# A list scheduler without same-engine waits, with another port rule and a margin on its costs, for a one-core RWKV and local-attention kernel

## The chip, the cores and the metric

The kernel runs on one core of one Trainium2 chip, in float32. The metric is the device time in microseconds (us) of one execution of the whole program. Each version is run several times and the median counts.

The core has five engines that matter here: TensorE (PE, matrix products and transposes), VectorE (DVE), ScalarE (ACT), GpSimd (POOL) and SyncE (SP, which issues all DMA transfers of this kernel). Each engine takes its instructions strictly in the order in which the program lists them, and waits on semaphores for the results of the others.

## The reference, cut to what matters

The input x is 2 x 4096 x 256. Two residual blocks follow each other. The first is an RWKV mixer: layer norm, three projections of a token-shifted input, a recurrence over the 4096 positions, a group norm, and an output projection.

```python
x = x + rwkv(layernorm(x))        # r, k, v projections, scan over time, group norm, W_o
x = x + ffn(layernorm(x))         # two layers of the following
```

Each of the two layers of the second block has local attention in windows of 128 positions, where a query sees its own and the previous window, and a gated feed-forward:

```python
h = shift_token(x)                          # second half of the channels one position later
q, k, v = split(h @ wqkv, 3)                # 8 heads of 64
q, k = rotary_xpos(l2norm(q) * qs, l2norm(k) * ksc)
o = softmax(mask(8 * q @ k_around.T)) @ v_around
x = x + o @ wo
h = layernorm(shift_token(x)) * lg + lb
a, g = split(h @ w1 + b1, 2)                # 682 hidden channels
x = x + (a * gelu(g)) @ w2 + b2
```

## The kernel before

The kernel is written as a recording. Every call such as `nc.vector.tensor_tensor(...)` does not emit an instruction; `note` (L230) stores it as an operation with its engine, its place in the recording and the earlier operations it depends on. `cost` (L294) gives each operation two figures: `step`, for how long it occupies its engine, and `time`, after which its result is there. It also sets `lock`, which says whether the operation takes the port that VectorE and GpSimd share. When all is recorded, `order` (L364) runs a list schedule over five engines and `give` (L490) emits the operations in the order of their planned starts. All real instructions therefore carry the line of that emission, L506, but for two forms of one operation: L500 (VectorE) and L502 (ScalarE).

`order` keeps for each engine a list of operations whose predecessors are planned. `ready` (L383) says when such an operation could start: after the planned end of each predecessor plus `SEM` = 60 ns. `earliest` (L393) raises this if the shared port is taken or if no PSUM bank is free. Of the operations that could start first on an engine (within 1 ns, L427), the one with the lowest priority key goes, and the key is the row at which the code placed it. The engine whose next start is earliest moves on. Operations recorded on the engine `either` (copies out of PSUM, and `scaled`, a multiplication by a number per partition) have no engine yet; they stand in the lists of both ScalarE and VectorE and go to whichever comes first. In the schedule before, two operations of one engine that depend on each other are also kept apart by the full `time` of the first plus 60 ns; other operations may be planned in between.

The work itself runs in three stages. First the recurrence of batch row 0 runs by itself, in chunks of 512 positions (`Recurrence`, L573: `ahead` loads, normalizes and projects a chunk; `scans`, L726, runs it over time). Then a loop (L1389) goes over 128 windows of 128 positions: 2 batch rows x 2 layers x 32 windows. Each turn n finishes window n and prepares window n+1. Four windows make a block of 512 positions, for which the feed-forward runs in large products. In the first 50 or so of the 128 turns the recurrence of batch row 1 is laid in between as 16 chunks of 256 positions, with its own row n + 0.5. So the first half of the loop carries more work of VectorE than the second.

The operations that the text refers to, by the names in the profile:

- `project` (L941) makes q, k and v of window n+1 (`bank<-wqkv,xT`). `norms` (L989) sums the squares (`rn<-sq`) and takes the inverse root on GpSimd (`rn<-rn,mhalf`); `cosines` (L997) and `rotated` (L1003) finish the rotation on VectorE (`sq<-qk,tab`, `sq<-sq,t`, `qk<-sq,rn`), and GpSimd makes the other part (`t<-qk,tab`).
- `transpose_qk` (L1014) transposes q and k on TensorE (`bank<-mats,qk`) in the next turn, before the scores (`bank<-kT,qT`).
- `softmax` (L1062) runs in four groups of two heads. It writes the scores of the own window over the masked ones of the previous window (`COPY_PREDICATED`) and takes the row extreme (`nmx<-bank`) on VectorE, the exponential with its sum on ScalarE (`pr<-bank,nmx`), then on VectorE the reciprocal of the sums (128x2), a 128x2 addition into the first columns (`pr<-pr`), and two `scaled` on `either` (`pr<-pr,sums`, 128x129).
- `transpose_p` (L1109) transposes the probabilities on TensorE (`bank<-mats,pr`), and `pT`, `pB` leave PSUM for the products with v.
- `output` (L1159) adds the result to x; `shift` (L1171) moves it by one position with DMAs on SP (`h<-x`); then the layer norm (`st`, `mv`, `rs`, `h<-h,mv,rs`), and `transpose_h` (L1196) once a block.

Of the kernel before, what the change touches and what calls it, by code (L numbers as in the profile page):

```python
# [54 lines left out]


SEM = 60
LOAD = 1283
TURN = {"row": 195, "col": 95, "full": 199}
SETS = {AF.Exp: 1, AF.Tanh: 1, AF.Gelu: 2, AF.Ln: 3}  # L60
# [98 lines left out]
class Op:  # L159
    __slots__ = (  # L160
        "eng", "name", "args", "kw", "step", "time", "deps", "after", "left", "at", "ready",
        "set", "lock", "ops", "banks", "uses", "passes", "half", "start", "end", "n", "ins", "outs",
    )


# [8 lines left out]
class Plan:  # L174
# [119 lines left out]
    def cost(self, o):  # L294

        views = [*o.outs, *o.ins]
        n = max([v.idx.size for v in views] or [1])
        psum = any(v.place.psum for v in views)
        wide = sum(v.idx.size > 16 and not v.place.psum for v in o.ins)
        o.set, o.lock, o.half, o.passes, name = None, False, "full", 0, o.name  # L300
        if o.eng == "tensor":
            trans = name == "transpose"
            left = o.args[1]
            move = o.args[2] if len(o.args) > 2 else o.args[1]
            cols = max(move.idx.size, left.idx.size) if not trans else P
            o.step = (1 if trans else 2) * (cols / 1.2 + (2 if cols >= 256 else 3))
            if not trans and left.shape[0] <= 64:
                o.half = "row"
            elif not trans and left.idx.size <= 64:
                o.half = "col"  # L310
            if o.half != "full":
                o.step /= 2
            o.time = o.step + 150
        elif o.eng == "vector":
            d = 150 + 1.04 * n
            if name == "tensor_tensor_reduce":
                d = 240 + 1.04 * n
            elif name == "tensor_tensor_scan":
                d, o.lock = 203 + 2.1 * n, True
            elif name == "scalar_tensor_tensor":  # L320
                d, o.lock = 200 + 1.05 * n, wide > 1
            elif name == "tensor_tensor":
                o.lock = wide > 1
            elif name == "tensor_scalar":
                d, o.lock = 155 + (1.27 if psum else 0.98) * n, not psum and n > 64
            elif name == "tensor_copy" and not psum:
                d, o.lock = 230 + 0.45 * n, n > 64
            elif name == "bn_aggr":
                d = 172
            elif name == "reciprocal":  # L330
                d = 147 + 4 * n
            o.step, o.time = max(d - 85, 60), d
        elif o.eng in ("scalar", "either"):
            d = (160 if psum else 195) + 0.83 * n
            if name == "scaled":
                d = 305 + 0.76 * n
            elif name == "activation":
                o.set = SETS.get(o.args[2])
                if o.args[2] == AF.Identity:
                    d = 365 + 0.87 * n  # L340
                elif isinstance(o.kw.get("bias"), View):
                    d += 85
            o.step, o.time = d - 100, d
            if "accum_out" in o.kw:
                o.time = d + 200
        elif o.eng == "gpsimd":
            o.lock = n > 64
            if name == "tensor_tensor":
                d = 430 + 156 * n if ALU.pow in o.args else 140 + 2.22 * n
            elif name == "tensor_scalar":  # L350
                d = 230 + 1.12 * n
            else:
                d = (100 if name == "memset" else 187) + 0.98 * n
            o.step, o.time = d, d
        else:
            v = min(views, key=lambda v: v.shape[0] * v.idx.size)
            size = 4 * v.shape[0] * v.idx.size
            rows = max(v.shape[0] if v.shape[0] > 1 else v.shape[1] for v in views)
            ways = max(k for k in range(1, 17) if rows % k == 0)
            o.passes = size / 170 if ways == 16 else size / (25 * ways)  # L360
            o.step, o.time = 60, 2000 + o.passes


    def order(self):  # L364
        owner = {}
# [11 lines left out]
        lock = dict.fromkeys(("vector", "gpsimd"), 0.0)  # L377
        waiting = {e: [] for e in engines}
        banks = [0.0] * 8
        counts = {}  # L380
        table, half, dma = 1, "full", 0.0

        def ready(g):  # L383
            t, off = 0.0, 0.0
            for o in g:
                for d in o.deps:
                    if owner[d] is not g:
                        t = max(t, d.end + SEM - off)
                off += o.step
            for e in ("scalar", "vector") if g[0].eng == "either" else (g[0].eng,):  # L390
                waiting[e].append((t, g))

        def earliest(e, t, g):  # L393
# [4 lines left out]
            if need:  # L398
                have = sorted(b for b in banks if b is not None)
                if len(have) < need:  # L400
                    return None
                t = max(t, have[need - 1] + SEM)
            return t
# [8 lines left out]
        while todo:  # L412
            for e in engines:
                if e not in stale:
                    continue
                best = None
                cands = []
                for t, g in waiting[e]:
                    s = earliest(e, t, g)
                    if s is not None:  # L420
                        cands.append((max(s, free[e]), g))
                if not cands:
                    pick[e] = None
                    continue
                t0 = min(s for s, _ in cands)
                for s, g in cands:
                    if s <= t0 + 1:  # L427
                        key = g[0].at
                        if best is None or key < best[0]:
                            best = (key, s, g)  # L430
                pick[e] = (best[1], best[2])
            stale = set()
            e = min((e for e in engines if pick[e]), key=lambda e: pick[e][0], default=None)
            assert e is not None, "no operation can start"
            t, g = pick[e]
            for o in g:
                if e == "tensor" and o.half != half:
                    t += TURN[o.half]
                    half = o.half
                if e == "scalar" and o.set not in (None, table):  # L440
                    t += LOAD
                    table = o.set
                for p in o.banks:
                    b = min((i for i in range(8) if banks[i] is not None), key=lambda i: banks[i])
                    p.bank, banks[b] = b, None
                    p.real = self.bank_tiles[b]
                    counts[p] = (len(p.users), 0.0)
                step, time = o.step, o.time
                if o.eng == "either" and e == "vector":
                    n = o.outs[0].idx.size  # L450
                    time = 150 + 1.04 * n if o.name == "copy" else 155 + 0.98 * n
                    step = time - 85
                    o.lock = o.name == "scaled"
                if o.eng == "either":
                    o.eng = e
                o.start = t
                if e == "sync":
                    dma = max(dma, t) + o.passes
                    o.end = max(t + time, dma + 2000)
                else:  # L460
                    o.end = t + time
                if o.lock and e in lock:
                    lock[e] = o.end
                t += step
                done.append(o)
                for p in o.uses:
                    c, last = counts[p]
                    counts[p] = (c - 1, max(last, o.end))
                    if c == 1:
                        banks[p.bank] = counts[p][1]  # L470
                        stale.add("tensor")
            free[e] = t
            if g[0].lock:
                stale.update(lock)
            stale.add(e)
            for x in engines:
                n = len(waiting[x])
                waiting[x] = [c for c in waiting[x] if c[1] is not g]
                if len(waiting[x]) != n:
                    stale.add(x)  # L480
            for nxt in after.get(id(g), ()):
                left[id(nxt)] -= 1
                if not left[id(nxt)]:
                    ready(nxt)
                    stale.update(("scalar", "vector") if nxt[0].eng == "either" else (nxt[0].eng,))
            todo -= 1
# [1058 lines left out]
```

## Time and profile before

| | |
|---|---|
| median of three runs | 3071.16 us (3068.86 to 3071.94) |
| the profiled execution | 3073.15 us, of which the profile's span is 3071.1 us |
| mean granted TensorE clock in it | 0.991 of full speed |
| TensorE busy, share of the span | 2968.5 us, 97% |
| VectorE | 2609.7 us, 85% |
| ScalarE | 1667.2 us, 54% |
| GpSimd | 1424.4 us, 46% |
| instructions | 48744 |

An engine is busy while an instruction of it runs; waiting on a semaphore does not count. A busy TensorE is not TensorE at its peak, since the ends of its pipelined products are modelled. The page of the profile also follows the chain of work that ended last back from the end, and the queries of the trace give the waits of each engine, the groups of instructions, and the instructions in order of time.

### The profile page before, as it was taken

How to read it: one execution, taken by the hardware profiler on the slowest of the kernel's cores; microseconds unless marked ns; L12 is line 12 of the kernel's file. 1: busy time of each engine (PE TensorE's matmuls, PEld its weight loads, DVE VectorE, ACT ScalarE, POOL GpSimd, SP SyncE). 2: the span in 40 equal slices, each digit the busy share in tenths (PEclk: the TensorE clock that was granted, in tenths of full speed). 3: DMA queues.
4: the chain of work that ended last, by engine and by line, in shares of the span. 5: the costliest groups of instructions: out<-in, count | busy, mean ns of one | idle time of the engine just before them, and what ended most of it. 6: DMA issues, size and time to landing. Idle time of an engine off the chain costs nothing.

```text
span 3071.1 us, 48744 instructions
## 1 busy us (share of the span) xinstructions
PE 2968.5 (97%) x15500; PEld 1914.7 (62%) x15500; DVE 2609.7 (85%) x5969; ACT 1667.2 (54%) x4485; POOL 1424.4 (46%) x1705
## 2 busy tenths in 40 slices
PE   9979999999999999999999999999999999999998
PEld 4456666666666666666666566666666666666665
DVE  7989988989889989898888888888888888888884
ACT  6866755556556566555445454445445445445443
POOL 3227544444445445545544444445444454454440
PEclk9989999999999999999999999999999999999999
DMA  2322112111112111111122221111112121111110
GB/s 82 111 89 68 55 48 64 58 52 49 59 59 66 64 56 59 51 55 50 51 66 78 70 71 58 58 58 56 49 46 69 60 63 56 53 52 55 47 42 24
DMA packets 178313, 182.49 MB, mean 59 GB/s; under 512 B 27044, under 2 KB 147716, under 8 KB 177544
## 3 DMA queue, kind: packets, MB, share of 16 engines
q1 hardware_dynamic: 178056, 179.38, 19.1%
q8 instruction: 123, 2.02, 0.3%
q14 instruction: 134, 1.10, 0.1%
HBM read 79.17 MB, written 33.55 MB: 37 GB/s over the span
## 4 chain that ended last, share of the span: by engine, by line
PE 64%; DVE 22%; ACT 6%; issue 3%; POOL 3%; DMA 1%; SPq 1%; DVEq 0%; ACTq 0%; POOLq 0%
PE bank L506 64%; DVE arena L506 4%; DVE qk L506 2%; ACT pr L506 2%; DVE sq L506 2%; DVE bank L506 2%; DVE rn L506 2%; DVE x L506 2%; DVE pr L500 1%; DVE nmx L506 1%; DVE pB L506 1%; POOL rn L506 1%; ACT L506 1%; ACT arena L506 1%; POOL rs L506 1%
## 5 line engine op out<-in xcount | busy, mean ns | idle before, releaser
L506 PE MATMUL bank<-wqkv,xT 128*128 128x512 f32 x1536 | 727.4, 599 | 0.0
L506 PE MATMUL bank<-hT,w 128*128 128x512 f32 (+1 forms) x1408 | 647.9, 594 | 1.1 <-ACT hT L506 1.1
L506 POOL TENSOR_TENSOR t<-qk,tab 128x256 f32<-128x256 f32 x512 | 379.2, 761 | 443.6 <-DVE qk L506 295.3
L506 ACT ACTIVATE pr<-bank,nmx 128x129 f32<-128x129 f32 (+1 forms) x1024 | 368.5, 375 | 280.6 <-DVE nmx L506 273.3
L506 PEld LDWEIGHTS bank<-hT,w 128*128 128x128 f32 (+1 forms) x1408 | 257.2, 190 | 256.6 <-issue 242.1
L506 PEld LDWEIGHTS bank<-wqkv,xT 128*128 128x128 f32 x1536 | 269.4, 192 | 229.9 <-issue 220.6
L506 POOL TENSOR_TENSOR rn<-rn,mhalf 128x16 f32<-128x16 f32 x128 | 398.0, 3110 | 10.2
L506 PE MATMUL bank<-w,hm 128*128 128x256 f32 x1280 | 288.5, 380 | 0.0
L506 PEld LDWEIGHTS bank<-w,hm 128*128 128x128 f32 x1280 | 242.6, 191 | 33.4 <-issue 1.0
L502 ACT ACTIVATE pr<-pr,sums 128x129 f32<-128x129 f32 (+1 forms) x606 | 225.2, 414 | 52.1 <-DVE pr L506 48.3
L506 PE MATMUL bank<-wo,oT 128*128 128x256 f32 x1024 | 250.0, 387 | 0.2
L506 PE MATMUL bank<-kT,qT 64*128 64x256 f32 (+1 forms) x2048 | 246.9, 381 | 0.0
L506 PEld LDWEIGHTS bank<-mats,pr 128*128 128x128 f32 x1148 | 133.6, 135 | 157.8 <-issue 63.3
L506 PEld LDWEIGHTS bank<-wo,oT 128*128 128x128 f32 x1024 | 188.1, 190 | 69.3 <-issue 35.3
L506 ACT ACTIVATION_READ_ACCUMULATOR pr<-bank,nmx 128x1 f32 x1024 | 217.1, 212 | 0.0
L506 DVE COPY_PREDICATED bank<-packs,bank 128x254 f32<-128x254 int32 x496 | 185.6, 419 | 32.5 <-PE bank L506 32.3
L506 PEld LDWEIGHTS bank<-kT,qT 64*128 64x128 f32 x2048 | 191.1, 187 | 31.8 <-issue 8.4
L506 POOL TENSOR_TENSOR tab<-tab,qks 128x256 f32<-128x256 f32 x128 | 105.2, 822 | 214.7 <-DMA tab<-in_c_rot_dram 201.0
L506 PE MATMUL bank<-pT,vt 128*64 128x128 f32 x2048 | 204.7, 280 | 0.0
L506 PE MATMUL bank<-mats,pr 128*128 128x128 f32 x1148 | 178.0, 276 | 22.4 <-ACT pr L502 15.3
L506 ACT ACTIVATE sq<-qk 128x1024 f32<-128x1024 f32 x128 | 136.0, 1063 | 114.2 <-DVE qk L506 113.1
L506 PE MATMUL bank<-pB,dv 128*64 128x128 f32 x1984 | 194.2, 273 | 3.6 <-DMA pB<-last 2.8
(151 smaller groups left out, 5678.2 us busy)
## 6 DMA issues: line engine op xcount, KB each, us to landing
vr<-vt SPq DMA_DIRECT2D x124, 224.0 KB
tab<-in_c_rot_dram SPq DMA_DIRECT2D x128, 128.0 KB
kT<-kT SPq DMA_DIRECT2D x64, 256.0 KB
z<-zd SPq DMA_DIRECT2D x16, 512.0 KB
x<-in_x_dram SPq DMA_DIRECT2D x16, 512.0 KB
x1d<-x SPq DMA_DIRECT2D x16, 512.0 KB
x<-x1d SPq DMA_DIRECT2D x16, 512.0 KB
h<-x SPq DMA_DIRECT2D x128, 64.0 KB
```

The costliest lines, as they stand in the source:

```text
L500: self.nc.vector.tensor_scalar(dst, src, scale, None, ALU.mult)
L502: self.nc.scalar.activation(dst, src, AF.Copy, scale=scale)
L506: getattr(getattr(self.nc, o.eng), name)(*args, **kw)
```

## The change

The change touches only the planner, not what is computed. It does five things:

1. `ready` counts only predecessors on other engines. An operation that depends on one of its own engine is planned directly behind it, without the 60 ns and without the part of `time` that lies beyond `step`. For `either` operations this is judged for each of the two engines separately.
2. The port rule of VectorE: a two-input operation takes the shared port if both inputs have the full size of the operation and lie in SBUF (before: if both have over 16 elements); one-input forms take it from 17 elements on (before: from 65).
3. The port rule of GpSimd: every operation but `memset` takes the port (before: those of over 64 elements), the small ones only for 100 ns (the new `hold`).
4. The port is held for `hold` from the start, which is the cost without the margin.
5. `SLACK` = 1.06: `step` and `time` of VectorE, ScalarE and GpSimd are multiplied by 1.06 in the plan. TensorE and SP keep theirs.

```diff
+SLACK = 1.06
...
-        wide = sum(v.idx.size > 16 and not v.place.psum for v in o.ins)
-        o.set, o.lock, o.half, o.passes, name = None, False, "full", 0, o.name
+        inside = sum(v.idx.size == n and not v.place.psum for v in o.ins)
+        o.set, o.lock, o.half, o.passes, name, hold = None, False, "full", 0, o.name, None
...
             elif name == "scalar_tensor_tensor":
-                d, o.lock = 200 + 1.05 * n, wide > 1
+                d, o.lock = 200 + 1.05 * n, inside > 1
             elif name == "tensor_tensor":
-                o.lock = wide > 1
+                o.lock = inside > 1
             elif name == "tensor_scalar":
-                d, o.lock = 155 + (1.27 if psum else 0.98) * n, not psum and n > 64
+                d, o.lock = 155 + (1.27 if psum else 0.98) * n, not psum and n > 16
             elif name == "tensor_copy" and not psum:
-                d, o.lock = 230 + 0.45 * n, n > 64
+                d, o.lock = 230 + 0.45 * n, n > 16
...
         elif o.eng == "gpsimd":
-            o.lock = n > 64
+            o.lock = name != "memset"
...
             o.step, o.time = d, d
+            hold = d if n > 64 else 100
...
+        o.hold = hold or o.time
...
         def ready(g):
-            t, off = 0.0, 0.0
-            for o in g:
-                for d in o.deps:
-                    if owner[d] is not g:
-                        t = max(t, d.end + SEM - off)
-                off += o.step
             for e in ("scalar", "vector") if g[0].eng == "either" else (g[0].eng,):
+                t, off = 0.0, 0.0
+                for o in g:
+                    for d in o.deps:
+                        if d.eng != e:
+                            t = max(t, d.end + SEM - off)
+                    off += o.step
                 waiting[e].append((t, g))
...
-                    o.lock = o.name == "scaled"
+                    o.lock, o.hold = o.name == "scaled", time
                 if o.eng == "either":
                     o.eng = e
+                if e not in ("tensor", "sync"):
+                    step, time = step * SLACK, time * SLACK
...
                 if o.lock and e in lock:
-                    lock[e] = o.end
+                    lock[e] = t + o.hold
```

More of the change, by code (lines that the diff above doesn't have):

```diff
@@ L161 @@
         "eng", "name", "args", "kw", "step", "time", "deps", "after", "left", "at", "ready",
-        "set", "lock", "ops", "banks", "uses", "passes", "half", "start", "end", "n", "ins", "outs",
+        "set", "lock", "hold", "ops", "banks", "uses", "passes", "half", "start", "end", "n", "ins", "outs",
     )
```

## The prediction

> **What bounds the kernel now.** I read the page first, for the shares of the engines and of the chain of work that ended last, then the same by stage.
>
> ```profile
> PE 2968.5 (97%) x15500; PEld 1914.7 (62%) x15500; DVE 2609.7 (85%) x5969; ACT 1667.2 (54%) x4485; POOL 1424.4 (46%) x1705
> ...
> PE 64%; DVE 22%; ACT 6%; issue 3%; POOL 3%; DMA 1%; SPq 1%; DVEq 0%; ACTq 0%; POOLq 0%
> ```
>
> TensorE is the bound by busy time, but the chain leaves it for a third of the span, and then it is mostly on VectorE. The windows show where (columns: length, then busy us and instructions by engine):
>
> ```profile
> 0.00:340.00 340.00, 308.28 (x1164) 181.05 (x1165) 297.66 (x625) 241.35 (x473) 143.28 (x213) 0.96 0.26 87
> 340.00:1400.00 1060.00, 1020.66 (x5462) 673.52 (x5461) 957.91 (x2190) 629.22 (x1662) 505.03 (x600) 0.99 0.19 56
> 1400.00:3000.00 1600.00, 1576.54 (x8603) 1021.30 (x8602) 1323.38 (x3089) 778.03 (x2308) 770.30 (x883) 1.00 0.19 58
> ```
>
> While the second recurrence lies between the windows (340 to 1400), VectorE is busy 957.91 of 1060 us, 90%; afterwards 83%. Added up by engine from the chain in order of time, VectorE holds 23% of the chain in the first stage (77 of 340 us), 38% in the second (402 us) and 12% in the third (185 us). An extra microsecond of VectorE is thus worth 0.23, 0.38 and 0.12 us, as long as the chain keeps its course.
>
> What TensorE waits for:
>
> ```profile
> PE bank L506 <- DVE qk L506: 31.1, 31, 2.9
> PE bank L506 <- ACT pr L502: 15.3, 22, 3.4
> ...
> PE bank L506 <- DVE h L506: 9.4, 3, 4.7
> ```
>
> This counts only full idleness. Comparing the starts of successive TensorE instructions with their undisturbed spacing (429 ns at 512 columns, 216 at 256, 109 at 128), I find 158 us lost, by what the late one waited for last: 39 for the q/k transposes (`qk`), 34 for the probabilities (`pr`, `scaled`), 20 for `h`, the rest spread. Of the 39, 18.6 fall on one of the four windows of a block (the second) after turn 56; of the 34, 32.5 on the fourth (21.5 before turn 56, 11.0 after).
>
> **What the Trainium skill says.** "VectorE: DVE Perf Modes", section "The DRAIN you can't avoid", holds that the semaphore between two VectorE operations costs nothing extra. This trace differs:
>
> ```profile
> 1773.49 0.35 DVE L506 TENSOR_TENSOR pr<-pr 128x2 f32<-128x2 f32 x1
> 1773.88 0.91 DVE L500 TENSOR_SCALAR pr<-pr,sums 128x129 f32<-128x129 f32 x2
> 1774.71 0.40 DVE L506 TENSOR_TENSOR x<-x,bank 128x256 f32<-128x256 f32 x1
> ```
>
> The `scaled` needs the addition and starts 0.04 us after its end; the addition to x needs neither and starts 0.08 us before the `scaled` ends. Over the trace the median is +35 ns for 187 adjacent dependent pairs and -83 ns for 4892 independent ones: **a dependent neighbour costs 117 ns of VectorE**. On ScalarE it is +32 against -94, 126 ns; the overlap is the "about 93 ns" of "ScalarE: Activation LUTs", section "What ACT_TABLE_LOAD costs". "SBUF — State Buffer", section "Who interferes with whom", says that a VectorE operation with two SBUF inputs and a GpSimd operation that reads SBUF block each other for the whole instruction. The trace agrees: the 128x2 addition takes 143 ns in the median with GpSimd quiet and up to 1112 ns beside it; such excess sums to 130 us.
>
> **The change part by part.** From the order in which the built programs' instructions stand:
>
> *Dependent neighbours on VectorE.* Adjacent dependent pairs go from 256 to 1529: 495 addition -> `scaled` (81 before), 467 `COPY_PREDICATED` -> reduce (none before), 199 statistics -> aggregate (47), and the steps of the recurrence. The plan used to put another instruction in between. 1273 more x 117 ns = 149 us of VectorE. By stage, cut where the TensorE work before them matches the windows: 174, 486 and 613 pairs, or 20.4, 56.9 and 71.7 us; by the chain shares 4.6 + 21.6 + 8.3 = **+34.5 us**. No trace here shows the pair with `COPY_PREDICATED`. Its bounds are 0 (the skill's page) and 187 ns (the slowest pair shown, addition to addition, +104); 117 is the value of most others. The ends move the total pairs' cost to 94 and 182 us, the sum to +22 and +42.
>
> *Who does the flexible work.* Net 324 `scaled` go from ScalarE to VectorE and 66 copies the other way. A `scaled` on VectorE holds it about 198 ns (281 undisturbed, less 83 of overlap), a copy 597: +64 - 39 = +25 us, nearly all after turn 56, at 0.12: **+3**. ScalarE: -324 x 294 ns + 66 x 490 = -63 us at its chain share of 6%: **-4**. Its 158 more dependent pairs x 126 ns = 20 us: **+1**. Below zero is possible here, as one hop from VectorE to ScalarE goes with each.
>
> *The port.* The 128x2 addition is now kept off GpSimd's time in the plan. It takes 193 ns in the mean against 143, 25 us in all. If half goes, at 22%: **-3**. At worst zero; at best all 130 us of excess at 22%, -29, but most of it is of kinds that both plans keep apart and that overlap all the same.
>
> *Cover.* TensorE's order hardly moves: 96% of adjacent pairs stay, and its turns between half and full array stay 392. But where it moves, it helps. For the second window of a block after turn 56, the TensorE work between `project` and the q/k transposes grows from 10.7 to 13.9 us in the mean, while the VectorE work from `rn` to `qk` grows from 6.8 to 8.9, so 1.1 us is won in 18 blocks; the median cover grows more, from 10.7 to 15.4. I take 13 of the 18.6 us as gone. For the probabilities of the fourth window the cover stays at 7.5 us in the median and VectorE's work before the last `scaled` shrinks from 7.3 to 6.0 us after turn 56 and from 7.2 to 6.8 before: 5 of 32.5. **-18.** The rest stands still or shrinks: in the other windows that VectorE work grows by 1.4 to 2.4 us with the same cover; that is part of the first item. What is late next is again `qk`, in the second stage, where cover grew by 0.6 us and work by 2.0 in the second window.
>
> *Moved at no cost.* The 1496 DMA issues of SP are the same; 64% stand elsewhere, nine in ten by at most three places. The DMAs `h<-x` and what queues behind them on SP hold 2% of the chain in the second stage; other work of TensorE hides them, and if that goes, one late landing costs the 1.95 us that it has in the chain, per block at most: 0 to +30, taken as 0. GpSimd does the same 1701 operations at 46%; it has 71 more dependent pairs at 120 ns, 9 us at a chain share of 3%. One more table load is 1.3 us on ScalarE at 54%. VectorE hides none of its own part in the second stage; elsewhere its idle time does.
>
> Sum: 34.5 + 3 - 4 + 1 - 3 - 18 = +13.5 us. The profiled execution took 3073.15 us (span 3071.1 and 2.05 around it) and lies 2.0 us above the median, within what runs differ. The sum goes onto the median: **3085 us**.
>
> **The rivals.**
>
> *Faster: the margin buys more than VectorE loses.* Place: the q/k and probability transposes, 73 us of loss. With producers planned 6% slow, TensorE's fillers stand where they are needed. For it: the longer cover after turn 56; VectorE is idle 15% of the span and can swallow pairs there. Against: in the second stage covers stay as they were. If half of the 73 us goes (-36) and two thirds of the pairs' +34.5 are swallowed (+11.5), with -3 for the rest: -27, **3044 us**. It decides once more than 31 of the 73 us are recovered with the rest as summed.
>
> *Much slower: VectorE becomes the bound in the second stage.* Per 100 us of TensorE work, its demand goes from 89 to 95 us there (operations and pairs), plus 4 of port excess: nearly level with TensorE. Then the pairs of this stage count in full, 57 instead of 22, the first stage's too (20 instead of 5), and the third stage's at a third (24 instead of 8): 35 + 15 + 16 = 66 on top of 13.5, **about 3151 us**. For it: 90% busy already. Against: the planner knows VectorE's load and put other work around it. It decides when VectorE is over 97% busy between 340 and 1400.
>
> *No difference.* Half-hidden pairs and the won cover cancel: **3071**. That the plan does not do what it says is excluded: the order did change as described.
>
> **How the numbers follow.** Runs of this kernel lie within 0.1%; 0.2%, some 6 us, is about what a measurement can tell from no change. The likeliest case (around 3085, its own range 3070 to 3105) has 0.45, much slower 0.15, faster 0.27, no difference 0.13. Slower: 0.43 of the likeliest and 0.15, 0.58. Faster 0.28, the same 0.14. The range leaves out a tenth at each end: 3042 to 3132 us; the low end takes in the faster case, the bounds of the pairs (-13 to +8) lie inside.
>
> **What would show it right or wrong.** In the profile after: dependent pairs at +34 ns on VectorE, and its busy time up by about 120 us (25 of work, and 83 ns of lost overlap for each pair; the +34 counts as idle), to about 2730 us; ScalarE down by some 90 us. VectorE's chain share above 22%, most in the second stage. TensorE's waits for `qk` after turn 56 well under half of what they were, and new ones before. Wrong: if `COPY_PREDICATED` -> reduce overlaps at -83 ns, or if the span is below 3065 us with the pairs there, which would mean that VectorE's added stalls lay in its idle time.

## The result, and the profile after

The changed kernel takes **3118.57 us** in the median of four runs (3117.54 to 3120.63), against 3070.01 us (3066.13 to 3071.94) for the kernel before in the same series: a ratio of 1.0161, 95% interval 1.0143 to 1.0178. It is 48.6 us slower. The forecast was 14 us slower.

All differences in us below are medians less the median of the kernel before on the same chip, which lay between 3070.01 and 3073.76.

The page of the kernel after, busy time of each engine and then the chain of work that ended last:

```profile
PE 2971.5 (95%) x15500; PEld 1913.3 (61%) x15500; DVE 2763.6 (89%) x6227; ACT 1655.5 (53%) x4228; POOL 1422.7 (46%) x1705
...
PE 46%; DVE 42%; issue 4%; ACT 3%; DMA 2%; SPq 2%; POOL 1%; DVEq 0%; POOLq 0%; ACTq 0%
```

TensorE does the same work in a longer span. VectorE is busy 154 us longer, and its share of the chain went from 22% to 42%. The windows at the same cuts as before (length, then busy us and instructions of PE, PEld, DVE, ACT and POOL, then the clock, DMA share and GB/s):

```profile
0.00:340.00 340.00, 297.29 (x1077) 174.10 (x1078) 297.59 (x604) 230.00 (x418) 111.34 (x188) 0.95 0.26 84
340.00:1400.00 1060.00, 1003.82 (x5388) 658.71 (x5386) 991.85 (x2221) 627.14 (x1575) 510.23 (x607) 0.99 0.18 55
1400.00:3000.00 1600.00, 1563.81 (x8528) 1013.26 (x8527) 1405.19 (x3246) 761.67 (x2142) 778.08 (x883) 1.00 0.19 57
```

VectorE is busy 93.6% of the second window and 87.8% of the third (90.4% and 82.7% before). Added up by engine and stage, VectorE now holds 36% of the chain up to 340 us, 53% from there to 1420 us and 37% from there to 3045 us, where it held 23%, 38% and 12%. Most of that growth is in the stage that had looked safe.

What TensorE waits for in the kernel after (line and engine that wait, what they wait for: us in total, times, longest):

```profile
PE bank L511 <- DVE qk L511: 43.7, 47, 2.8
PE bank L511 <- DVE pr L505: 36.2, 37, 3.2
...
PE bank L511 <- DVE h L511: 8.6, 4, 3.6
...
PE bank L511 <- ACT pr L507: 0.4, 1, 0.4
```

`qk` grew from 31.1 to 43.7 us, and the wait for probabilities that VectorE scales (now L505, L500 before) from 5.3 to 36.2. Part of the second is a change of engine: the wait for those that ScalarE scales (now L507, L502 before) fell from 15.3 to 0.4, so the two together went from 20.6 to 36.6. By the spacing of TensorE's starts its loss went from 158 to 202 us, most of the 48.6.

The forecast had no sight of `COPY_PREDICATED` next to the reduce that needs it. VectorE's instructions in order of time in the kernel after (start us, duration us):

```profile
1805.38 0.43 DVE L511 COPY_PREDICATED bank<-packs,bank 128x254 f32<-128x254 int32 x1 [0.72 <-PE bank L511]
1805.84 0.43 DVE L511 TENSOR_REDUCE nmx<-bank 128x2 f32<-128x258 f32 x1
1806.18 0.42 DVE L511 COPY_PREDICATED bank<-packs,bank 128x254 f32<-128x254 int32 x1
1806.63 0.43 DVE L511 TENSOR_REDUCE nmx<-bank 128x2 f32<-128x258 f32 x1
```

The first copy ends at 1805.81 and its reduce starts 0.03 us later; the next copy, which needs nothing of that reduce, starts 0.09 us before the reduce ends. Over the trace 467 such pairs have a median gap of +34 ns, 199 `bn` pairs (statistics -> aggregate) +34, 495 pairs addition -> `scaled` +35, 107 pairs of the large products and additions of the rotation (`sq<-qk,tab` -> `sq<-sq,t` -> `qk<-sq,rn`) some +104, and independent neighbours -83. So the 149 us of lost time on VectorE that the prediction summed are there (1273 more pairs at 117 ns); open was what they are worth.

The groups of `pr` in the kernel after (form, count, then busy us and mean ns of one, then idle time just before them and its releaser):

```profile
L505 DVE TENSOR_SCALAR pr<-pr,sums 128x129 f32<-128x129 f32 x718 | 219.3, 332 | 17.5
L507 ACT ACTIVATE pr<-pr,sums 128x129 f32<-128x129 f32 x274 | 110.4, 404 | 143.3 <-DVE pr L511 138.5 <-DVE pr L505 1.0
L511 DVE TENSOR_TENSOR pr<-pr 128x2 f32<-128x2 f32 x496 | 83.4, 168 | 0.0
```

The choice of engine is the one that the prediction read from the order (718 of the 128x129 `scaled` on VectorE, 406 before), and the 128x2 addition fell from 193 to 168 ns, half of its excess, as taken.

### The profile page after: what moved, and what is told of

It is laid out like the page before. It is cut to its first block, busy times and chain, and to the rows that moved or that the text cites. A ratio compares the mean times of both kernels' runs of the same rounds, so it can differ in the third digit from the quotient of the medians.

```text
span 3116.5 us, 48622 instructions
## 1 busy us (share of the span) xinstructions
PE 2971.5 (95%) x15500; PEld 1913.3 (61%) x15500; DVE 2763.6 (89%) x6227; ACT 1655.5 (53%) x4228; POOL 1422.7 (46%) x1705
## 3 DMA queue, kind: packets, MB, share of 16 engines
q1 hardware_dynamic: 178056, 179.38, 18.6%
## 4 chain that ended last, share of the span: by engine, by line
PE 46%; DVE 42%; issue 4%; ACT 3%; DMA 2%; SPq 2%; POOL 1%; DVEq 0%; POOLq 0%; ACTq 0%
PE bank L511 46%; DVE sq L511 6%; DVE arena L511 5%; DVE pr L505 4%; DVE nmx L511 4%; DVE bank L511 4%; DVE qk L511 3%; DVE rn L511 2%; DVE pB L511 2%; DVE x L511 2%; DMA h<-x 2%; SPq L511 2%; DVE pT L511 1%; DVE hm L511 1%; DVE h L511 1%
## 5 line engine op out<-in xcount | busy, mean ns | idle before, releaser
L511 POOL TENSOR_TENSOR t<-qk,tab 128x256 f32<-128x256 f32 x512 | 400.5, 802 | 475.7 <-DVE qk L511 278.4
L511 POOL TENSOR_TENSOR rn<-rn,mhalf 128x16 f32<-128x16 f32 x128 | 379.1, 2962 | 10.3
L505 DVE TENSOR_SCALAR pr<-pr,sums 128x129 f32<-128x129 f32 (+1 forms) x740 | 226.0, 332 | 18.0
L511 PEld LDWEIGHTS bank<-wo,oT 128*128 128x128 f32 x1024 | 187.0, 190 | 69.2 <-issue 30.1
L511 DVE TENSOR_REDUCE nmx<-bank 128x2 f32<-128x258 f32 x496 | 211.3, 426 | 15.9
L511 DVE COPY_PREDICATED bank<-packs,bank 128x254 f32<-128x254 int32 x496 | 207.1, 418 | 16.2 <-PE bank L511 15.8
L511 POOL TENSOR_TENSOR tab<-tab,qks 128x256 f32<-128x256 f32 x128 | 111.6, 873 | 231.3 <-DMA tab<-in_c_rot_dram 215.8
L511 PE MATMUL bank<-mats,pr 128*128 128x128 f32 x1148 | 176.2, 276 | 39.1 <-DVE pr L505 36.2
L511 PEld LDWEIGHTS bank<-kT,qT 64*128 64x128 f32 x2048 | 191.0, 187 | 32.5 <-issue 7.4
L511 ACT ACTIVATION_READ_ACCUMULATOR pr<-bank,nmx 128x1 f32 x1024 | 206.8, 202 | 0.0
```

The source lines that it names most:

```text
L505: self.nc.vector.tensor_scalar(dst, src, scale, None, ALU.mult)
L511: getattr(getattr(self.nc, o.eng), name)(*args, **kw)
```

## The experiments

The theories: **price** (the pairs cost what was summed, but a microsecond of VectorE is worth more than its chain share of before); **engines** (what hurts is that VectorE does 324 more `scaled`); **order** (the plan moved work to worse places, whatever the pairs cost); **port and margin** (these parts lose). "Pairs" below are dependent neighbours on VectorE in the order: 256 before, 1529 after; `scaled` on VectorE: 424 and 748.

### Which part does it: the parts one by one

**e1_ready**: part 1 alone, as an edit of the kernel before.

```diff
-            t, off = 0.0, 0.0
...
-                    if owner[d] is not g:
-                        t = max(t, d.end + SEM - off)
...
             for e in ("scalar", "vector") if g[0].eng == "either" else (g[0].eng,):
+                t, off = 0.0, 0.0
...
+                        if d.eng != e:
+                            t = max(t, d.end + SEM - off)
```

> The kernel before with the first part of the change alone: operations of one engine no longer wait for each other in the plan; old port rules, no margin. Dependent neighbours on VectorE: 1498 (before 256, after 1529). Theory 'pairs' (each dependent neighbour stalls VectorE 117 ns, and that is the loss): 3110 to 3130 us. Rival 'rules' (the new port rules and the margin delay the 128x2 additions and what follows, and that is the loss): within 10 us of before, 3060 to 3080 us. Rival 'choice' (the 324 'scaled' that VectorE takes over are the loss; here they move too, 744 on VectorE): 3110 to 3130 us as for 'pairs', so this run does not tell these two apart.

**e2_port**: parts 2 to 4 alone. **e4_waits_back**: parts 2 to 5, so the changed kernel with only `ready` as it was. Both have this edit to the kernel after, and e2 also `SLACK = 1.0`:

```diff
+            t, off = 0.0, 0.0
+            for o in g:
+                for d in o.deps:
+                    if owner[d] is not g:
+                        t = max(t, d.end + SEM - off)
+                off += o.step
             for e in ("scalar", "vector") if g[0].eng == "either" else (g[0].eng,):
-                t, off = 0.0, 0.0
...
-                        if d.eng != e:
-                            t = max(t, d.end + SEM - off)
```

> The kernel before with the new port rules alone; same-engine waits planned as before, no margin. Dependent neighbours on VectorE: 214. Theory 'pairs': 3062 to 3078 us. Rival 'rules': 3085 us or more. The port excess of the 128x2 addition (25 us before) should fall if the rule does what it says.

> The changed kernel with the first part alone undone: the new port rules and the margin stay, same-engine waits are planned as before. Dependent neighbours on VectorE: 140; 417 'scaled' on VectorE. Theory 'pairs': 3050 to 3072 us, no slower than before and perhaps faster, since the margin and the cover stay. Rival 'rules': 3095 us or more. Rival 'choice': 3050 to 3075 us.

**e3_slack**: part 5 alone, as an edit of the kernel before.

```diff
+SLACK = 1.06
...
+                if e not in ("tensor", "sync"):
+                    step, time = step * SLACK, time * SLACK
```

> The kernel before with the margin alone (steps and times of VectorE, ScalarE and GpSimd times 1.06 in the plan), old port rules. Dependent neighbours on VectorE: 215. From e2 (port rules alone, 24 us faster) and e4 (both, 54 us faster), if the two add up: 30 us faster than before, 3042 us (3030 to 3055). If the margin only helps with the right port rules: 3060 to 3075 us.

| kernel | median us | ratio (95%) | difference | pairs | `scaled` on VectorE |
|---|---|---|---|---|---|
| e1, waits removed alone | 3129.86 | 1.0190 (1.0175 to 1.0206) | +57.7 | 1498 | 744 |
| e2, port alone | 3047.90 | 0.9921 (0.9907 to 0.9936) | -24.2 | 214 | 359 |
| e3, margin alone | 3033.91 | 0.9875 (0.9860 to 0.9889) | -39.8 | 215 | 457 |
| e4, port and margin | 3017.98 | 0.9824 (0.9809 to 0.9838) | -54.2 | 140 | 417 |
| the whole change | 3118.57 | 1.0161 (1.0143 to 1.0178) | +48.6 | 1529 | 748 |

Part 1 does all the damage and the other parts gain, so "port and margin" falls. e2 and e4 came out faster than any of the theories written down for them allowed. Part 1 costs more beside them (from -54.2 to +48.6: 103 us) than alone (58 us). With the waits kept, port and margin gain 54 us; with the waits removed, from +57.7 to +48.6, only 9.

The planner also works out how long it believes its order will take (`self.length` at the end of `order`). For the change this is 2959 us, for e4 2965; for e1 2942, for the kernel before 2947. So without the waits the planner believes that it gains 4 to 6 us, and the chip takes 58 and 103 us more. What is lost is time that the plan does not know of. The page of e4:

```profile
PE 2953.4 (98%) x15500; PEld 1907.4 (63%) x15500; DVE 2553.7 (85%) x5920; ACT 1692.0 (56%) x4534; POOL 1439.4 (48%) x1705
...
PE 77%; DVE 14%; ACT 4%; DMA 2%; issue 2%; SPq 1%; POOL 0%; DVEq 0%; POOLq 0%; ACTq 0%
```

And TensorE's waits in it:

```profile
PE bank L511 <- ACT arena L511: 16.5, 8, 7.4
PE bank L511 <- DVE qk L511: 13.9, 10, 4.1
...
PE bank L511 <- DVE pr L505: 1.7, 3, 1.1
```

The waits for `qk` and for `pr` from VectorE, 43.7 and 36.2 us after the whole change, are 13.9 and 1.7 here, though VectorE is as busy as before the change (85%).

### Pairs or engines

**e8_after_choice_of_e4** and **e9_e4_choice_of_after** exchange the engines: the planner of one kernel, with each `either` operation bound to the engine it has in the other.

```diff
+        if eng == "either":
+            o.pin = ("vector" if PINS[self.pinned] == "1" else "scalar",)
+            self.pinned += 1
...
-            for e in ("scalar", "vector") if g[0].eng == "either" else (g[0].eng,):
+            for e in g[0].pin or (g[0].eng,):
```

> The changed kernel's planner (no same-engine waits, new port rules, margin), but each copy and each 'scaled' is pinned to the engine that it has in e4_waits_back: 417 'scaled' on VectorE instead of 748. Dependent neighbours on VectorE: 1307. After e7 took away 1108 pairs for 14 us alone, two theories are left for the other 85 us or so between e4 (3018) and the changed kernel (3118). Theory 'choice' (331 more 'scaled' load VectorE with some 100 us): 3025 to 3050 us. Theory 'order' (the plan takes chains on VectorE as some 100 ns a step shorter than they are, so its starts on TensorE come too early and other work is pushed behind whole chains): 3090 to 3115 us.

> The planner of e4_waits_back (same-engine waits, new port rules, margin), but each copy and each 'scaled' is pinned to the engine that it has in the changed kernel: 748 'scaled' on VectorE instead of 417. Dependent neighbours on VectorE: 119. Theory 'choice': 3080 to 3105 us, most of the way to the changed kernel although the waits are planned. Theory 'order': 3018 to 3035 us.

e8 took 3076.82 us (1.0012, 1.0005 to 1.0019; +3.1 us, 1307 pairs, 417 `scaled`), e9 3023.31 us (0.9842, 0.9827 to 0.9857; -50.4 us, 119 pairs, 748 `scaled`). The engines (the copies move with the `scaled`) cost 4 us where pairs are few (e4 to e9) and 46 where they are many (e8 to the change). As a cause of their own they fall; on top of the pairs they count. e9 lies where "order" had put it, e8 in neither range, between the two.

These runs give the price twice over, at equal engines. From e4 to e8 come 1167 pairs, 137 us of VectorE, and 57.3 us of time: 0.42 us for each. From e9 to the whole change come 1410 pairs, 165 us, and 99.0 us of time: 0.60. The order differs too between these kernels, so this alone doesn't part "price" from "order".

### The price by itself

**e16_before_stalls** and **e17_e4_stalls** were to load VectorE with nothing else changed: the order stays, and two one-element memsets stand ahead of each operation that is the second of a new pair after the change (965 places in the kernel before, 1019 in e4).

```diff
         for o in self.done:
+            if o.eng == "vector" and PLACES >> o.n & 1:
+                for _ in range(2):
+                    self.nc.vector.memset(pads[count % 8], 0.0)
+                    count += 1
```

> The kernel before, its schedule untouched, with two one-column memsets on VectorE put ahead of 965 of its operations: those on VectorE that stand directly behind a predecessor in the changed kernel and not here. This loads VectorE with some 110 us more (965 x 2 x 57 ns, the spacing behind a 128x2 operation), as the stalls of dependent neighbours do, without moving anything else. Theory 'stalls' (VectorE's lost time is what costs, at near its full price in the crowded half): 3105 to 3130 us. Theory 'order' (lost time is cheap, as the chain shares of before had it at 0.23 to 0.38, and the rest of the change's loss lies in the order): 3085 to 3100 us.

> The same two memsets ahead of 1019 operations of e4_waits_back (3018 us), some 116 us more on VectorE. Theory 'stalls': 3075 to 3105 us, which would be most of the 100 us between e4 and the changed kernel. Theory 'order': 3030 to 3055 us.

They took 3078.04 us (1.0025, 1.0016 to 1.0033) and 3022.14 us (0.9841, 0.9826 to 0.9855), +7.4 us against before, and a difference 5.7 us above that of e4. Both lie below all that was expected of them. But nothing was priced, because the load did not arrive. VectorE in order of time in e16:

```profile
1786.26 0.42 DVE L569 TENSOR_REDUCE nmx<-bank 128x2 f32<-128x258 f32 x1
1786.33 0.06 DVE L556 MEMSET pad<- 128x1 f32 x2
1786.61 0.42 DVE L569 TENSOR_REDUCE nmx<-bank 128x2 f32<-128x258 f32 x1
```

The memsets run while the reduce ahead of them still runs. 1930 of them add 11 us to VectorE's busy time (2620.9 against 2609.7).

**e19_before_held** makes the load depend: ahead of 844 of the same places in the kernel before stands a reduce of two elements of the output that VectorE has just written (94 places before turn 0, 393 up to turn 55, 357 later). It must wait as a pair does.

```diff
+            if o.eng == "vector" and PLACES >> o.n & 1:
+                v = last.outs[0]
+                part = v[(slice(None), *[0] * (v.idx.ndim - 1), slice(0, 2))].get()
+                self.nc.vector.tensor_reduce(pads[count % 8], part, AX.X, ALU.max)
...
+            if o.eng == "vector":
+                last = o
```

> The kernel before, its schedule untouched, with a reduce of two elements of the predecessor's output to one put on VectorE ahead of 844 of its operations (94 before the loop, 393 in turns 0 to 55, 357 later). Each has to wait for its predecessor, as a dependent neighbour does (117 ns), and then takes some 58 ns itself, so VectorE loses about 148 us, as much as the prediction gave the 1273 pairs. The memsets of e16 began under the operation ahead of them and loaded VectorE with 11 us only, so they priced nothing. Theory 'stalls' (the lost time is what costs): 3110 us or more. Theory 'order' (the price from the chain shares of before is right, 34.5 us for 149, and the rest of the loss lies in the order): 3095 to 3108 us. Below 3090 us: lost time on VectorE is cheaper still, and nearly all of the loss is order.

It took 3151.47 us (1.0255, 1.0238 to 1.0273), +78.0 us. VectorE in order of time in e19:

```profile
1802.77 1.20 DVE L572 TENSOR_TENSOR qk<-sq,rn 128x1024 f32<-128x1024 f32 x1
1804.01 0.15 DVE L557 TENSOR_REDUCE pad<-qk 128x1 f32<-128x2 f32 x1
1804.08 0.17 DVE L572 BATCH_NORM_AGGREGATE mv<-st 128x2 f32<-128x6 f32 x1
```

The reduce starts 0.04 us after the multiplication has ended, and the next operation starts 0.07 us after the reduce has started. In the medians these are +34 and 72 ns, where the next operation would have started 83 ns before the end: 189 ns a place, 844 x 0.189 = 160 us of VectorE. 78 us for 160: **a microsecond of VectorE is worth 0.49 us** in an order that is not touched at all. (Reduces that read PSUM also hold its bank a little longer; that is in the 0.49.) TensorE's waits in e19:

```profile
PE bank L572 <- DVE qk L572: 49.4, 35, 3.6
PE bank L572 <- ACT pr L568: 24.5, 39, 3.4
```

They are the same two as before the change, each about 60% longer (31.1 and 15.3 before). The chain shares of before, weighted with the stages of the 844 places (0.23, 0.38, 0.12), say 0.25. So "price" is shown without any change of order, for lost time that the plan did not know of. "Order" does not fall with that: how the two share the loss in the changed order is not parted by this run.

### Can the pairs be taken out, or planned for

**e7_apart**: the schedule of the change, in which the second of a pair is afterwards set one place later on its engine, where dependencies and banks allow it.

```diff
-        return sorted(done, key=lambda o: (o.start, o.n))
+        return self.apart(sorted(done, key=lambda o: (o.start, o.n)))
```

> The changed kernel's own schedule, every choice of engine kept (748 'scaled' on VectorE), but after planning each dependent neighbour on VectorE or ScalarE is set one place later on its engine where nothing forbids it. Dependent neighbours on VectorE: 421 instead of 1529. Theory 'pairs': 1108 of 1273 pairs go, so about 42 of the 48.6 us come back: 3070 to 3085 us. Rival 'choice': the moves of one place change nothing of it, 3105 to 3120 us. Rival 'rules': 3105 to 3120 us.

**e14_margin_113_apart** does the same to e11 (below).

> As e11 (changed kernel with a margin of 1.13 on VectorE, 3049 us), and each dependent neighbour on VectorE or ScalarE then set one place later where nothing forbids it, as in e7. Dependent neighbours on VectorE: 353 instead of 1370. If what is left between e11 and e4 (31 us) is the stall of the pairs itself: 3020 to 3032 us. If it is the order in which the chains stand: 3040 to 3055 us.

e7 took 3104.40 us (1.0104, 1.0087 to 1.0121), only 16 us less than the change by the differences, with 421 pairs in place of 1529: 0.13 us for each microsecond of pairs taken out, where "pairs" had expected 42 us back. e14 took 3088.31 us (1.0055, 1.0040 to 1.0070) with 353 pairs, 42 us *more* than e11 with 1370 by the differences, and outside both ranges expected of it. Fewer pairs are no gain by themselves. A likely reason: where the second operation stands on a chain, another operation of some hundred ns put before it delays it more than 117 ns. That last reading is argued from the durations; it was not tried by itself.

**e5_measured** keeps the wait of an operation for one of its own engine in the plan, to the planned end of that one plus the gap that the trace shows (34 ns on VectorE, 32 on ScalarE), in place of 60 ns.

```diff
+OWN = {"vector": 34, "scalar": 32, "gpsimd": 0}
...
+                        elif owner[d] is not g and e in OWN:
+                            t = max(t, d.end + OWN[e] - off)
```

> The changed kernel, but an operation waits in the plan for a predecessor on its own engine as the trace shows it: to the predecessor's end plus 34 ns on VectorE and 32 ns on ScalarE (the changed kernel: no wait; the kernel before: end plus 60 ns). Dependent neighbours on VectorE: 130; 456 'scaled' on VectorE. Every theory that puts the loss down to leaving these waits out: 3005 to 3030 us, as e4 (3018). If it were the 60 ns that helped, above 3040 us.

3031.63 us (0.9866, 0.9852 to 0.9881) with 130 pairs: the gain is back but for 12 us (e4 has -54.2, this -42.1). So most of what the waits gain does not hang on the 60 ns. **e10_true_times_pinned** and **e13_true_times_free** instead choose without the wait, as the change does, and only then move the planned start of what was chosen behind the wait; e10 with the engines of the change, e13 free.

```diff
+                if e in OWN:
+                    t = max([t, *(d.end + OWN[e] for d in o.deps if d.eng == e)])
```

> The changed kernel with the same engine for each copy and 'scaled' (748 'scaled' on VectorE), and with operations still chosen as if those of one engine never waited for each other; but once one is chosen, the plan charges the wait: it starts no earlier than its predecessor on its own engine ends plus 34 ns (VectorE) or 32 ns (ScalarE). Dependent neighbours on VectorE: 1403, nearly as in the changed kernel (1529); e9, with the same engines and planned waits, has 119 and takes 3023 us. Theory 'times' (the plan's clock for VectorE runs ahead of the chip, so everything planned against it comes too early): 3030 to 3055 us, though the pairs stay. Theory 'whole chains' (VectorE runs a chain to its end while other work stands behind it, whatever the plan's clock says): 3090 to 3120 us.

> As e10 (operations chosen as if those of one engine never waited, but the plan's clock charges the wait once they are chosen), with the engine of each copy and 'scaled' left to the plan: 624 'scaled' and 589 copies on VectorE (changed kernel 748 and 662). Dependent neighbours on VectorE: 1402. Theory 'clock' (the loss is a plan whose VectorE runs ahead of the chip; e10 stayed at 3096 because it had to keep the engines chosen under the false clock): 3045 to 3070 us, near e11 (3049). Theory 'whole chains' (chains run to their end): 3085 to 3105 us, near e10.

3096.01 us (1.0075, 1.0060 to 1.0090) and 3095.93 us (1.0082, 1.0067 to 1.0097), with some 1400 pairs each. A clock that charges the waits after the choice wins back some 25 us of 103. **e11_margin_113** gives VectorE the missing time as a larger margin, 1.13 in place of 1.06.

```diff
-                    step, time = step * SLACK, time * SLACK
+                    s = 1.13 if e == "vector" else SLACK
+                    step, time = step * s, time * s
```

> The changed kernel with a margin of 1.13 instead of 1.06 for VectorE alone. 1389 pairs more than in e4, at 117 ns, are 163 us, 6.8% of VectorE's 2423 us of issue, so this puts the missing time back into the plan, spread evenly. Dependent neighbours on VectorE: 1370. Theory 'times': 3040 to 3070 us. Theory 'whole chains': 3095 to 3120 us.

3049.29 us (0.9923, 0.9908 to 0.9938), with 1370 pairs. Busy time and chain on its page:

```profile
PE 2957.7 (97%) x15500; PEld 1914.3 (63%) x15500; DVE 2660.5 (87%) x6064; ACT 1719.0 (56%) x4390; POOL 1416.2 (46%) x1705
...
PE 73%; DVE 17%; ACT 6%; issue 2%; DMA 1%; SPq 1%; POOL 1%; DVEq 0%; POOLq 0%; ACTq 0%
```

VectorE has 17% of the chain, although nearly all pairs are there; 73 of the 103 us are back. The order also takes work off VectorE: 63 `scaled` and 100 copies fewer than in the change, about 72 us by the prediction's 198 and 597 ns. But e13 takes off nearly as much (124 `scaled` and 73 copies, about 68 us) and stays at +25 us, so this alone is not what brings e11 back. More likely the clock of the change had no room: its margin of 1.06 is used up by stalls of about that size (149 us on 2610 is 5.7%), and most of the loss goes once VectorE is planned slower. e10 and e13, which charge each stall where it falls, win back much less. For e10 the planner's own clock says it: its order lasts 3021 us there, 61 more than that of the change and 42 more than that of e11 (2979), nearly all of the 47 us between the two kernels. The choice ignores waits that the plan then has to sit through. For e13 (2990) this makes 11 of the 49 us; the rest stays open. e10 and e13 lie in the range of "whole chains", e11 in that of its rival "times", so neither theory holds for all three.

### A faster version

With the waits kept, the margin was varied.

```diff
-SLACK = 1.06
+SLACK = 1.10
```

**e12_e4_margin_110**, **e15_e4_margin_115** and **e18_e4_margin_108** are e4 with 1.10, 1.15 and 1.08.

> The version with the same-engine waits kept (e4_waits_back, 3018 us) with a margin of 1.10 instead of 1.06. If the margin still gains as it did from 1.0 to 1.06 (30 us at the new port rules): 3000 to 3012 us. If 1.06 covers what the chip adds (130 us of port excess on 2397 us of VectorE issue are 5.4%): 3013 to 3030 us.

> The version with the same-engine waits kept and the new port rules, with a margin of 1.15 (1.06: 3018 us, 1.10: 3001 us). If the margin still gains: 2985 to 2998 us. If it is past its best: 3003 to 3020 us.

> The version with the same-engine waits kept and the new port rules, margin 1.08 (1.06: 3018 us, 1.10: 3001 us, 1.15: 3046 us). If the time is smooth in the margin: 3005 to 3015 us. If single schedules scatter: anything from 2990 to 3045 us.

e12, e15 and e18 took 3000.91 us (0.9764, 0.9748 to 0.9780), 3046.45 us (0.9919, 0.9902 to 0.9935) and 3012.39 us (0.9810, 0.9795 to 0.9824). From 1.0 over 1.06, 1.08, 1.10 to 1.15 the times are 3048, 3018, 3012, 3001 and 3046. **e12 is the fastest kernel of this study, 2.4% under the kernel before.** The page of e12:

```profile
PE 2945.1 (98%) x15500; PEld 1914.6 (64%) x15500; DVE 2556.1 (85%) x5886; ACT 1718.4 (57%) x4569; POOL 1435.4 (48%) x1705
...
PE 88%; DVE 7%; ACT 3%; DMA 1%; issue 1%; SPq 1%; POOL 0%; POOLq 0%; DVEq 0%; ACTq 0%
```

TensorE has 88% of the chain, VectorE 7%. The step from 1.10 to 1.15 costs over 45 us, and lies outside what was expected, so the margin is a setting to be searched and no law of it follows from five points.

## Why the prediction was right or wrong

**Right: the sign, the mechanism and its amount on VectorE.** The pairs stand where the order said, `COPY_PREDICATED` -> reduce among them, at +34 ns; VectorE's busy time rose by 154 us where about 120 were named (the two terms given for it, 25 us and 83 ns for each of 1273 pairs, add up to 131); its chain share rose, and is largest in the second stage. On the cost of a semaphore between VectorE operations, the trace after differs from "VectorE: DVE Perf Modes", section "The DRAIN you can't avoid", as the one before did: all 1529 pairs have a median gap of +35 ns, independent neighbours -83. What the prediction calls addition to addition, at +104, are the products and additions of the rotation; `COPY_PREDICATED` -> reduce is not near that bound.

**Wrong: the price, the step that failed.** The place and the amount of the lost time were right; the term of the sum that was mis-sized is what it is worth. The prediction multiplied 149 us by chain shares of the old profile, "as long as the chain keeps its course", to +34.5 us: 0.23 on average. e19 measures 0.49 with the order untouched, which makes 73 us; e4 against e8 gives 0.42 and e9 against the change 0.60. The chain did not keep its course: the third stage was priced at 0.12 and VectorE ended with 37% of the chain there. A likely reading is that a chain share prices only a small addition, and that with each further microsecond more waits of TensorE end with VectorE, which was 83 to 90% busy and got 6% more load. No run tries this with smaller loads. Nor is 0.49 a price for every order: where the plan knows of the work, 331 more `scaled` for 24 copies (e4 to e9, about 51 us of VectorE) cost 4 us. The engine choice's 25 us, priced at 0.12 too, come to 12 at 0.49 instead of 3; e9 and e8 show that they cost between 4 and 46, by the pairs beside them.

**With the price put right the sum is too high**, 73 + 12 - 4 + 1 - 3 - 18 = +61 us against 48.6. In e1, part 1 brings 1242 pairs (145 us) and about 29 us more issue, and costs 57.7 us: 0.33 a microsecond, less than in e19. What its order wins in return was not isolated.

**Right in place, wrong as a balance: the cover.** By the spacing of TensorE's starts, the loss at the second window's q/k transposes after turn 56 fell from 18.6 to 7.1 us, 11.5 of the 13 forecast. For the probabilities of the fourth window it fell from 32.5 to 12.8, 20 in place of 5. But new losses came at places with little or no loss before: q/k of the fourth window from 4.1 to 30.1 us, probabilities of the first from 1.0 to 26.2, of the third before turn 56 from 0.3 to 10.7. The step that failed here is "The rest stands still or shrinks", with what it lost taken as "part of the first item". In the order, the VectorE work from `rn` to `qk` of the fourth window after turn 56 grew from 9.8 to 13.2 us, while the TensorE work that covers it shrank from 21.3 to 16.7, both in the mean (the median of the cover did not move); both could be read before. This is not the whole cause: counted by the plan's step times, which give 9.3 to 12.4 and 20.2 to 16.1 us for these, e4's order has 11.6 of work and 17.8 of cover at the same windows and loses 0.5 us there, the changed order 17.3. So the sign named for it was half right: waits for `qk` after turn 56 as a whole did not halve, they went from 21 to 24 us.

**Mis-sized: the port and the margin.** -3 for the port and -18 for the cover were taken; port and margin are worth -54 with the waits kept (e4) and -9 with them removed (e1 to the change). The rival "the margin buys more than VectorE loses" was thus right on the margin's worth: e3 wins 40 us by it alone. It lost, as e11 suggests, because the unplanned stalls use up the margin. The addition's excess fell by the expected half, 25.9 to 12.8 us, but VectorE's excess over undisturbed durations rose in all from 130 to 159 us: the 1024-element addition into `sq` alone went from 0.9 to 22.2. What "SBUF — State Buffer", section "Who interferes with whom", says of the lock agrees with it; which operations it meets depends on the whole order, and the prediction looked at one form.

**Misread: the ScalarE sign.** "Down by some 90 us" holds for the busy times of its groups of instructions added up (1993 to 1905 us, 89 less), and the durations one by one fell by 121 (2060 to 1939). The page's busy time, which the sign reads like, fell by 12 alone, from 1667.2 to 1655.5: it counts overlapping neighbours once, and fewer overlap now.

**The rival "VectorE becomes the bound in the second stage"** did not come about: VectorE is 93.6% busy there, under the 97% that it named. The time lies between its 3151 and the forecast, as the measured price lies between the chain shares and one.

## What to carry to other kernels

Price lost time on a nearly full second engine by a load test (dependent dummies at the places concerned in the old order), not by its share of the old profile's chain: here the shares said 0.25 at those places and the test 0.49. It is the price of time that the plan does not know of; work that the plan knew of cost far less here. In a planner, keep the true waits and put a margin on top: removing the waits cost 58 us alone, and took 45 of the 54 us that port rules and margin had to give. When cover moves, compute cover less work at every window and place, above all at those that show no wait yet.

## What the runs showed of the hardware that was not expected

- A VectorE memset without an input does not queue behind the operation ahead: in e16 the first of two starts 405 ns before that one's end in the median, and the second 8 ns after the first. As a load it failed here.
- A dependent reduce of two elements, whose record lasts 155 ns, costs 189 ns of VectorE in e19: the 83 ns of overlap that are lost, 34 until it starts and 72 until the next operation does.
- The dependent products and additions of the rotation (512 and 1024 elements, both inputs in SBUF) have a median gap of +104 ns on 107 pairs of the trace after, three times that of the other pairs. The 128x2 ones among themselves have +34. Why is open.
